# Destination scores of two graph-attention layers: spread over the partitions by two transfers through memory instead of by TensorE transposes

## The chip, the cores and the metric

The kernel runs on one core of a Trainium2 chip. A core has five engines with queues of their own: TensorE (PE, matrix products and transposes), VectorE (DVE), ScalarE (ACT), GpSimd (POOL) and SyncE (SP, which here only issues transfers). They work out of SBUF, an on-chip memory of 128 partitions; TensorE writes into the eight banks of PSUM, 2 KB a partition each; inputs and outputs lie in HBM, and 16 DMA engines move data between HBM and SBUF. An engine executes its own queue in order and waits on semaphores for the others.

The metric is the time of one execution on the device in microseconds (us).

## The reference

Four layers of graph attention are applied to 32 graphs of 512 nodes with 256 channels, all in float32, with one adjacency matrix for all. Each layer ends in a residual and a layer norm.

```python
# layer 0 ("a" in the kernel): additive attention, one head
h = x @ W
s1 = einsum('bnf,f->bn', h, a1);  s2 = einsum('bnf,f->bn', h, a2)
e = leaky_relu(s1[:, :, None] + s2[:, None, :], 0.2)
attention = softmax(where(adj > 0, e, NEG_BIG), axis=-1)
x = layernorm(x + elu(attention @ h))
# layer 1 ("b"): transformer block, 8 heads of 32 channels, masked dot-product attention
# layer 2 ("c"): additive attention again, 4 heads of 64 channels
e = e_src[:, :, None, :] + e_dst[:, None, :, :]       # each of shape (graph, node, head)
e = where(e >= 0, e, 0.2 * e);  attn = softmax(where(mask, e, NEG_INF), axis=2)
x = layernorm(x + elu(einsum('bijh,bjhd->bihd', attn, q)))
# layer 3 ("d"): bilinear attention, e = leaky_relu((x W1) (x W2)^T), then relu
```

In layers a and c the score of a pair is a sum: one number of the source node i plus one number of the destination node j. In a tile with 128 sources on the partitions and 512 destinations along the free dimension, the source's number is one value a partition. The destination's is a whole row of 512 values that every partition needs alike. How this row gets onto all partitions is what is changed.

## The kernel before

**Tiling.** A graph's 512 nodes are four blocks of 128 (`NB`), taken in two halves (`F`). The projection `prepare` (L733) yields `v`, with nodes on partitions: 256 channels, then a source score and a destination score per head. Destination score of head h is the column `C + H + h` of `v`.

**Layers a and c** (`Gat.attend`, L741). For each head the column of each node block is given to TensorE as a broadcast operand (128 equal columns) and transposed against the identity (L752 to L757): four transposes fill a PSUM bank `dst` [128, 512], whose rows are all the same. `masked` (L637) on VectorE then makes, for each of the four source blocks, `t = dst + neg`, with `neg` the bfloat16 mask in SBUF, and the row maximum. `leaky_softmax` adds the source score and applies the slope (L666) and the exponential (L672) on ScalarE. The tiles `t` are transposed on TensorE (`turn`, L549), copied from PSUM (`copied`, L492 on ScalarE or L494 on VectorE, as the planner decides), and multiplied with `v`: L807 in layer a and d, L561 in layers b and c.

**Forms of the TensorE array.** L561 uses column tiles 32 or 64 wide ("columns"), L853 (scores of layer b) row tiles of 32 ("rows"), everything else the full array ("full").

**Order.** No engine's order is written by hand. Each piece of work is given to `Plan.op` with its cost per engine, what it writes and reads, and a `lag`. `Plan.order` runs a list scheduler over all of them with up to four graphs in flight (`WINDOW`), starts on each engine the fitting piece with the best key, and emits the instructions in that order. The key is made of the graph's age (`AGE`), the length of the work behind it, an urgency by engine and stage (`URGENT`; "c3" is stage 3 of layer c) and, on TensorE, a weight for a change of form (`SWITCH`, `SWITCH_WEIGHT`). Buffers have a tag and a number of slots (`BUFS`); a piece starts only when its slots are free. `port=True` keeps a VectorE piece from starting while the planner thinks GpSimd is busy; of the VectorE pieces only the layer norms' last step (L621) has it.

**GpSimd** does residual additions (L629), the power for the norms (L609) and three additions or products of layer b (L914, L915, L918). **SyncE** issues all transfers: weights at the start, then for each graph two halves of `xT`, one `x` (L340) and two output stores (L1041).

Of the kernel before, what the change touches and what calls it, by code (L numbers as in the profile page):

```python
# [14 lines left out]
ALU = mybir.AluOpType  # L15
AX = mybir.AxisListType
PSUM = bass.MemoryType.PSUM

# [4 lines left out]
SLOPE = 0.2  # L25


BUFS = dict(t=18, pT=8, x=6, xT=3, v=5, qk=4, y=5, e=2, n=2, nT=2, hT=2, oT=4, small=8)


WINDOW = 4
# [5 lines left out]

AGE = {"PE": 51, "ACT": 138, "DVE": -107, "POOL": 461, "SP": 20}  # L40
URGENT = {
    "PE": {"a0": -417, "a1": 491, "a2": -867, "b0": -448, "b1": 197, "b2": 839, "c0": -557, "c1": -258, "c2": 203, "d0": -909, "d1": -511, "d2": -1186, "a3": 1287, "a4": 1218, "b3": -47, "b4": 169, "c3": 2234, "c4": 712},
    "ACT": {"a0": -671, "a1": 422, "a2": 770, "b0": 459, "b1": 253, "b2": 93, "c0": 729, "c1": 136, "c2": -360, "d0": 573, "d1": -523, "d2": -1234, "a3": 806, "a4": -162, "b3": 370, "b4": 340, "c3": 698, "c4": -390},
    "DVE": {"a0": -247, "a1": 1195, "a2": 496, "b0": 1368, "b1": 273, "b2": -132, "c0": -1160, "c1": 19, "c2": 666, "d0": -845, "d1": -1056, "d2": -1458, "a3": 1297, "a4": 438, "b3": -527, "b4": 175, "c3": 138, "c4": 1482},
    "POOL": {"a0": -896, "a1": -817, "a2": 582, "b0": 3, "b1": -713, "b2": 227, "c0": -148, "c1": -607, "c2": 1624, "d0": 582, "d1": 1022, "d2": -1512, "a3": -446, "a4": 431, "b3": 270, "b4": 1342, "c3": 708, "c4": 734},
    "SP": {},
}

SWITCH = {"full": {"rows": 0.1, "columns": 0.1}, "rows": {"full": 0.12, "columns": 0.12}, "columns": {}}
SWITCH_WEIGHT = 661


S_HEADS = 4
# [42 lines left out]
class Plan:  # L99
# [7 lines left out]
    def op(self, where, issue, writes=(), reads=(), takes=(), lag=0.0, port=False, form="full"):  # L107

        o = Op(len(self.ops), self.graph, where, issue)
        o.lag = LATENCY + lag
        o.port, o.form = port, form
        o.stage = self.stage
        self.ops.append(o)
        for buf in takes:
            if not buf.users and buf.tag is not None:
                o.takes.append(buf)  # L120
                self.bufs.append(buf)
                buf.users.append(o)
        for what, write in [(w, True) for w in writes] + [(r, False) for r in reads]:
            buf, cells = what if isinstance(what, tuple) else (what, None)
            if not buf.users and buf.tag is not None:
                o.takes.append(buf)
                self.bufs.append(buf)
            if not buf.users or buf.users[-1] is not o:
                buf.users.append(o)
            for c in range(len(buf.writer)) if cells is None else [cells]:  # L130
                if buf.writer[c] is not None:
                    o.after.add(buf.writer[c])
                if write:
                    o.after.update(buf.readers[c])
                    buf.writer[c], buf.readers[c] = o, []
                else:
                    buf.readers[c].append(o)
        o.after.discard(o)

    def order(self):  # L140
# [85 lines left out]
        while events:  # L226
# [28 lines left out]
            for e in URGENT:  # L255
# [3 lines left out]
                for o in ready.get(e, {}).values():  # L259
                    key = o.graph * AGE[e] - o.rank - URGENT[e].get(o.stage, 0)  # L260
                    if e == "PE":
                        key += SWITCH_WEIGHT * SWITCH[form].get(o.form, 0.0)
                    key = key, o.n
# [29 lines left out]
def gnn_stack(  # L293
# [4 lines left out]
    nc = tc.nc  # L298
    B, N, C = x.shape
    P = 128  # L300
    NB = N // P
    NC = C // P
    H1, D1 = 8, C // 8
    H2, D2 = 4, C // 4
# [6 lines left out]
    work = ctx.enter_context(tc.tile_pool(name="work", bufs=2))  # L311
    small = ctx.enter_context(tc.tile_pool(name="small", bufs=8))
    psum = ctx.enter_context(tc.tile_pool(name="psum", bufs=8, space=PSUM))


    plan = Plan()
    op = plan.op
    PE, ACT, DVE, POOL, SP = "PE", "ACT", "DVE", "POOL", "SP"
# [4 lines left out]
        return b  # L323

    def buf(tag, shape, name, cells=1, dtype=F32):
        return Buf(work, shape, tag, BUFS[tag], name, cells, dtype)

    def tiny(tag, shape, name, cells=1):
        return Buf(small, shape, tag, BUFS["small"], name, cells)

    def bank(shape, name, cells=1):
        return Buf(psum, shape, "ps", 8, name, cells)

    def block(i):
        return slice(i * P, (i + 1) * P)
# [9 lines left out]
    ident = const.tile([P, P], F32, name="ident")  # L345
# [141 lines left out]
    def copied(n, dst, ps, writes, reads):  # L487


        def issue(e):  # L490
            if e == ACT:
                nc.scalar.copy(dst(), ps())  # L492
            else:
                nc.vector.tensor_copy(dst(), ps())  # L494

        op({ACT: 0.03 + n * 0.00087, DVE: 0.06 + n * 0.00106}, issue, writes, reads)
# [57 lines left out]
    def weighted(pv, oT, pTs, v, lo, D, us):  # L554

        def issue(e):
            for j in range(NB):
                for h, pT in enumerate(pTs):  # L560
                    nc.tensor.matmul(  # L561
                        pv[h * D : (h + 1) * D], lhsT=v[:, j, lo + h * D : lo + (h + 1) * D],
                        rhs=pT[:, j], start=(j == 0), stop=(j == NB - 1), skip_group_check=True,
                    )

        op({PE: us}, issue, [pv], [v] + pTs, [oT], form="columns")
# [66 lines left out]
    def masked(s, t, top, at, i):  # L633


        def issue(e):
            nc.vector.tensor_tensor_reduce(  # L637
                out=t[:], in0=s[:], in1=neg[:, i], scale=1.0, scalar=LOWEST, op0=ALU.add,
                op1=ALU.max, accum_out=top[(slice(None),) + at],
            )  # L640

        op({DVE: 0.61}, issue, [t, top], [s, (neg, i)])
# [73 lines left out]
    class Gat(Layer):  # L716
# [24 lines left out]
        def attend(self):  # L741
            H, D, name, v = self.H, C // self.H, self.name, self.v
            G = min(H, P // D) if H > 1 else 1
            for g in range(0, H, G):
                ts = {}
                for h in range(G):
                    dst = bank([P, N], f"{name}_dst{g}{h}")
                    for i in range(NB):
                        ts[h, i] = buf("t", [P, N], f"{name}_t{g}{h}{i}")


                    def issue(e, at=C + H + g + h, dst=dst):  # L752
                        for j in range(NB):
                            column = v[:, j, at : at + 1].to_broadcast([P, P])
                            nc.tensor.transpose(dst[:, block(j)], column, ident)  # L755

                    op({PE: 0.44}, issue, [dst], [v], [ts[h, i] for i in range(NB)])  # L757
                    if h == 0:
                        tops = [
                            tiny("top", [P, FB, G], f"{name}_top{g}{f}") for f in range(F)  # L760
                        ]
                    for i in range(NB):
                        masked(dst, ts[h, i], tops[i // FB], (i % FB, slice(h, h + 1)), i)
                for f in range(F):
                    plan.stage = name[0] + "3"
                    pTs, inv = leaky_softmax(
                        {(h, i): ts[h, f * FB + i] for h in range(G) for i in range(FB)},
                        tops[f], v, C + g, G, f, f"{name}_{g}_{f}",
                    )
                    y = self.part_y(f)  # L770
                    plan.stage = name[0] + "4"
                    if H > 1:
                        pv = bank([P, FN], f"{name}_pv{g}{f}")
                        oT = buf("oT", [P, 1, FN], f"{name}_oT{g}{f}")
                        weighted(pv, oT, pTs, v, g * D, D, 1.86)
                        copied(FN, lambda oT=oT: oT[:, 0], lambda pv=pv: pv[:], [oT], [pv])
                        ps = turned_back(oT, 1, y, f"{name}_{g}{f}")
                        op({DVE: 0.4}, scaled(y, 0, g * D, ps, inv, D), [y], [ps, inv])
                    else:
                        pv = bank([P, FB, C], f"{name}_pv{f}")  # L780
                        rows_weighted(pv, pTs[0], v, y)
                        op({DVE: 0.62}, scaled(y, 0, 0, pv, inv, C), [y], [pv, inv])
                    plan.stage = name[0] + "1"
                    if g + G == H:
                        yield f
# [308 lines left out]
```

## Time and profile before

| | |
|---|---|
| Median of 3 runs | 3526.07 us (3525.98 to 3526.36) |
| Profiled execution | 3525.66 us, its span 3523.9 us |
| Granted TensorE clock in it | 0.999 |
| L755, the transposes of destination scores | 640 |
| L549, the transposes of the softmax tiles | 7168 matmuls, 898.4 us busy |
| L637, masking in layers a, c and d | 768, 685 ns median |
| L867, masking in layer b | 1024, 649.0 us busy |
| L492 and L494, copies of softmax tiles | 1099 on ACT, 693 on DVE |
| GpSimd busy | 869.1 us, 25% |

The span reaches from the first to the last record of the profiled execution. A share in percent is of the span. Busy shares overlap, since the engines work side by side; the chain of waits is followed back from the last instruction and tells what the end waited for. In lists of groups, `ps<-ident,v` means: written `ps`, read `ident` and `v`; `x640` is the number of instructions.

### The profile page before, as it was taken

The numbers are of one execution on the slowest core, as the hardware profiler recorded it, in microseconds if no ns is written. First come the engines' busy times: TensorE is split into PE (matmuls) and PEld (weight loads), VectorE is DVE, ScalarE is ACT, GpSimd is POOL, SyncE is SP. The second block draws the span as 40 slices with busy tenths as digits, with TensorE's granted clock in tenths as the row PEclk, the third lists the DMA queues.
The fourth block names the chain that finished last, engine by engine and source line by source line (L and its number), as shares of the span: only waits on it lengthen the run. The fifth ranks groups of instructions, "written<-read, shape, count | busy, mean of one in ns | idle before, by whom it ended". The sixth has DMA issues, their size and how long they took to land.

```text
span 3523.9 us, 68878 instructions
## 1 busy us (share of the span) xinstructions
PE 3501.5 (99%) x24728; PEld 2685.4 (76%) x24728; DVE 2973.8 (84%) x8792; ACT 2807.6 (80%) x6856; POOL 869.1 (25%) x840
## 2 busy tenths in 40 slices
PE   8999999999999999999999999999999999999999
PEld 7777777778777787877878778687787877878777
DVE  7789888888888888888888888888888888888886
ACT  6798877878788787887888878887788877888786
POOL 1222222222222222222222222222222222222322
PEclk9999999999999999999999999999999999999999
DMA  3000100001000010000100001000010000100000
GB/s 95 7 2 1 37 1 19 19 1 37 1 19 19 1 37 1 19 19 1 37 1 19 19 1 37 1 19 19 1 37 1 19 19 1 37 1 19 19 7 19
DMA packets 56918, 59.41 MB, mean 17 GB/s; under 512 B 3968, under 2 KB 55808, under 8 KB 56576
## 3 DMA queue, kind: packets, MB, share of 16 engines
q1 hardware_dynamic: 56576, 55.00, 4.9%
q8 instruction: 196, 3.21, 0.4%
q14 instruction: 146, 1.20, 0.1%
HBM read 38.21 MB, written 16.78 MB: 16 GB/s over the span
## 4 chain that ended last, share of the span: by engine, by line
PE 99%; DVE 1%; ACT 0%; DMA 0%; issue 0%; SPq 0%; POOLq 0%; POOL 0%; DVEq 0%
PE ps L549 23%; PE ps L561 13%; PE ps L520 13%; PE ps L807 12%; PE ps L535 10%; PE ps L853 8%; PE ps L733 7%; PE ps L975 6%; PE ps L505 3%; PE ps L755 2%; PE ps L575 2%; DMA xT<-in_x_T 0%; SPq L340 0%; DVE st L603 0%; DVE rstd L606 0%
## 5 line engine op out<-in xcount | busy, mean ns | idle before, releaser
L549 PEld LDWEIGHTS ps<-ident,t 128*128 128x128 f32 x7168 | 805.5, 141 | 178.4 <-issue 38.7
L549 PE MATMUL ps<-ident,t 128*128 128x128 f32 x7168 | 898.4, 274 | 1.0 <-ACT t L874 0.8
L874 ACT ACTIVATE t<-t,low 128x512 f32<-128x512 f32 x1024 | 734.8, 735 | 41.5 <-DVE low L867 41.5
L492 ACT COPY pT<-ps 128x512 f32<-128x512 f32 x1099 | 594.1, 593 | 119.9 <-PE ps L549 116.4
L867 DVE CUSTOM_DVE_ANT_0 t<-ps,neg 128x512 f32<-128x512 f32 x1024 | 649.0, 686 | 46.2 <-PE ps L853 43.6
L629 POOL TENSOR_TENSOR y<-y,x 128x512 f32<-128x512 f32 x256 | 330.0, 1290 | 1371.7 <-DVE y L586 493.3
L609 POOL TENSOR_TENSOR rstd<-rstd,mhalf 128x2 f32<-128x2 f32 x384 | 297.2, 774 | 1049.1 <-DVE rstd L606 934.3
L637 DVE CUSTOM_DVE_ANT_0 t<-ps,neg 128x512 f32<-128x512 f32 x768 | 492.3, 683 | 69.9 <-PE ps L975 59.4
L672 ACT ACTIVATE t<-t,bias 128x512 f32<-128x512 f32 x768 | 544.0, 709 | 0.4
L561 PE MATMUL ps<-pT,v 128*32 128x256 f32 (+1 forms) x6144 | 486.1, 382 | 0.0
L494 DVE COPY pT<-ps 128x512 f32<-128x512 f32 x693 | 451.3, 682 | 40.1 <-PE ps L549 37.8
L807 PE MATMUL ps<-v,pT 128*128 128x256 f32 x2048 | 465.5, 379 | 0.0
L666 ACT ACTIVATE t<-t,v 128x512 f32<-128x512 f32 x640 | 418.4, 715 | 32.5 <-DVE top L637 32.4
L561 PEld LDWEIGHTS ps<-pT,v 128*32 128x32 f32 (+1 forms) x6144 | 260.4, 118 | 208.1 <-issue 22.6
L807 PEld LDWEIGHTS ps<-v,pT 128*128 128x128 f32 x2048 | 378.5, 190 | 48.2 <-issue 2.3
L853 PE MATMUL ps<-qk,qk 32*128 32x512 f32 x2048 | 291.7, 639 | 0.0
L603 DVE BATCH_NORM_STATS2 st<-y 128x6 f32<-128x256 f32 x768 | 285.2, 413 | 4.5 <-POOL y L629 3.1
L975 PE MATMUL ps<-xT,qk 128*128 128x512 f32 x512 | 241.7, 596 | 0.0
L520 PE MATMUL ps<-xT,w_qkv_sb 128*128 128x256 f32 x1024 | 230.8, 379 | 0.0
L617 DVE TENSOR_SCALAR x<-y,mv,rstd 128x256 f32<-128x256 f32 x512 | 219.3, 474 | 3.7 <-POOL rstd L609 1.9
L874 ACT ACTIVATION_READ_ACCUMULATOR t<-t,low 128x1 f32 x1024 | 214.3, 209 | 0.0
L586 DVE TENSOR_TENSOR y<-ps,inv 128x512 f32<-128x512 f32 (+1 forms) x256 | 140.9, 551 | 83.9 <-PE ps L807 72.0
(84 smaller groups left out, 4630.4 us busy)
## 6 DMA issues: line engine op xcount, KB each, us to landing
xT<-in_x_T SPq DMA_DIRECT2D x64, 256.0 KB, 3.2
x<-in_x SPq DMA_DIRECT2D x32, 512.0 KB, 4.5
out<-x SPq DMA_DIRECT2D x64, 256.0 KB, 2.2
t<-in_adj SPq DMA_DIRECT2D x4, 256.0 KB, 6.8
w_qkv_sb<-in_L_gnn_w_qkv SPq DMA_DIRECT2D x1, 768.0 KB, 7.2
w_sb<-in_L_gnn_w SPq DMA_DIRECT2D x2, 256.0 KB, 5.8
t<-in_L_gnn_W SPq DMA_DIRECT2D x2, 256.0 KB, 2.8
w_sb<-in_L_gnn_W SPq DMA_DIRECT2D x1, 256.0 KB, 2.8
```

The lines of the kernel that those rows point to most:

```text
L492: nc.scalar.copy(dst(), ps())
L494: nc.vector.tensor_copy(dst(), ps())
L520: nc.tensor.matmul(ps[:, c], lhsT=w[:, k, lo + c * P : lo + (c + 1) * P], rhs=xT[:, k, nlo : nlo + FN], start=(k == 0), stop=(k == NC - 1),)
L549: nc.tensor.transpose(ps[:, j], t[:, block(j)], ident)
L561: nc.tensor.matmul(pv[h * D : (h + 1) * D], lhsT=v[:, j, lo + h * D : lo + (h + 1) * D], rhs=pT[:, j], start=(j == 0), stop=(j == NB - 1), ...
L637: nc.vector.tensor_tensor_reduce(out=t[:], in0=s[:], in1=neg[:, i], scale=1.0, scalar=LOWEST, op0=ALU.add, op1=ALU.max, accum_out=top[(sli ...
L672: nc.scalar.activation(t[:], t[:], AF.Exp, bias=bias[:, i, h : h + 1], accum_out=total[:, i, h : h + 1])
L807: nc.tensor.matmul(pv[:, i], lhsT=pT[:, j, block(i)], rhs=v[:, j, 0:C], start=(j == 0), stop=(j == NB - 1),)
L853: nc.tensor.matmul(s[:], lhsT=q_sb[at, c, block(f * FB + i)], rhs=k_sb[at, c], start=True, stop=True,)
L867: nc.vector.tensor_tensor_reduce(out=t[:], in0=s[:], in1=neg[:, f * FB + i], scale=-1.0 / math.sqrt(D1), scalar=HIGHEST, op0=ALU.add, op1= ...
L874: nc.scalar.activation(t[:], t[:], AF.Exp, bias=low[:, i, h : h + 1], scale=-1.0, accum_out=total[:, i, h : h + 1],)
L975: nc.tensor.matmul(s[:], lhsT=hh[:, k, block(f * FB + i)], rhs=xT[:, k], start=(k == 0), stop=(k == NC - 1),)
```

## The change

- `attend` makes a tile `row` [4, 512] in DRAM (HBM) for each graph and layer. For each head, SyncE writes the column of destination scores out of `v` into one row of it, value by value (512 values of 4 bytes from 128 partitions).
- A second transfer reads that row onto all 128 partitions of a tile `dst` [128, 512], which now lies in SBUF, with three slots. It waits until the write has landed. `masked` reads this `dst`; the instruction is otherwise the same.
- The transposes of L755 and their PSUM bank are gone. The buffers `t` are claimed by the masking and no longer by the transposes.
- The planner books both transfers on SP with 0.45 us and a lag of 3.0 and 2.5 us. A buffer's list of users now also has pieces that name an already used buffer in `takes`.
- `t` has 15 slots instead of 18, `nT` 3 instead of 2, `row` 37. The reserve that is kept in SBUF for transfers that GpSimd issues is 1024 bytes a partition, given explicitly. GpSimd issues no transfers in either kernel.
- All weights of the planner (`AGE`, `URGENT`, `SWITCH_WEIGHT`) are other numbers, so the order of all work on all engines is another one.

```diff
+DRAM = bass.MemoryType.DRAM
...
-BUFS = dict(t=18, pT=8, x=6, xT=3, v=5, qk=4, y=5, e=2, n=2, nT=2, hT=2, oT=4, small=8)
+BUFS = dict(t=15, pT=8, x=6, xT=3, v=5, qk=4, y=5, e=2, n=2, nT=3, hT=2, oT=4, dst=3, row=37, small=8)
...
-AGE = {"PE": 51, "ACT": 138, "DVE": -107, "POOL": 461, "SP": 20}
+AGE = {"PE": 215, "ACT": 489, "DVE": -131, "POOL": 484, "SP": 84}
...
-SWITCH_WEIGHT = 661
+SWITCH_WEIGHT = 1043
+
+DMA_US = 0.45
+ROW_LAG = 3.0
...
             if not buf.users and buf.tag is not None:
                 o.takes.append(buf)
                 self.bufs.append(buf)
+            if not buf.users or buf.users[-1] is not o:
                 buf.users.append(o)
...
+    dram = ctx.enter_context(tc.tile_pool(name="dram", bufs=1, space=DRAM))
...
-        return Buf(work, shape, tag, BUFS[tag], name, cells, dtype)
+        return Buf(dram if tag == "row" else work, shape, tag, BUFS[tag], name, cells, dtype)
...
         def attend(self):
             H, D, name, v = self.H, C // self.H, self.name, self.v
             G = min(H, P // D) if H > 1 else 1
+
+            row = buf("row", [H2, N], f"{name}_row", H)
+            for h in range(H):
+
+                def write(e, h=h):
+                    with nc.allow_non_contiguous_dma(reason="one score of each node"):
+                        nc.sync.dma_start(
+                            out=row[h].rearrange("(i p) -> p i", p=P), in_=v[:, :, C + H + h]
+                        )
+
+                op({SP: DMA_US}, write, [(row, h)], [v], lag=ROW_LAG)
             for g in range(0, H, G):
                 ts = {}
                 for h in range(G):
-                    dst = bank([P, N], f"{name}_dst{g}{h}")
+                    dst = buf("dst", [P, N], f"{name}_dst{g}{h}")
                     for i in range(NB):
                         ts[h, i] = buf("t", [P, N], f"{name}_t{g}{h}{i}")

-                    def issue(e, at=C + H + g + h, dst=dst):
-                        for j in range(NB):
-                            column = v[:, j, at : at + 1].to_broadcast([P, P])
-                            nc.tensor.transpose(dst[:, block(j)], column, ident)
-
-                    op({PE: 0.44}, issue, [dst], [v], [ts[h, i] for i in range(NB)])
+                    def read(e, h=g + h, dst=dst):
+                        nc.sync.dma_start(out=dst[:], in_=row[h].partition_broadcast(P))
+
+                    op({SP: DMA_US}, read, [dst], [(row, g + h)], lag=2.5)
...
-    nc = bacc.Bacc("TRN2", target_bir_lowering=False, num_devices=1)
+    nc = bacc.Bacc("TRN2", target_bir_lowering=False, num_devices=1, dynamic_dma_scratch_size=1024)
```

## The prediction

> **What bounds the kernel now.** I read the page first: busy shares, then the chain.
>
> ```profile
> span 3523.9 us, 68878 instructions
> ...
> PE 3501.5 (99%) x24728; PEld 2685.4 (76%) x24728; DVE 2973.8 (84%) x8792; ACT 2807.6 (80%) x6856; POOL 869.1 (25%) x840
> ...
> PE 99%; DVE 1%; ACT 0%; DMA 0%; issue 0%; SPq 0%; POOLq 0%; POOL 0%; DVEq 0%
> ...
> q1 hardware_dynamic: 56576, 55.00, 4.9%
> ```
>
> PE is busy all the time and the chain of waits lies on it: what leaves PE's queue leaves the time, as long as its suppliers keep up. The DMA engines are nearly empty. Next, the chain in order of time, from 1000 us on (start, length, line, matmuls):
>
> ```profile
> 1005.41 0.44 PE ps L755 x4
> ...
> 1006.28 1.88 PE ps L561 x16
> 1008.16 1.92 PE ps L520 x8
> ...
> 1015.19 1.73 PE ps L520 x8
> ...
> 1027.36 3.60 PE ps L561 x32
> ```
>
> L755 is what the change removes: 0.44 us for four transposes. The rest shows a second price. Two L561 groups (64-column tiles) in a row take 3.60, one alone 1.88; so a group is 1.72 and going in costs 0.16. L520 takes 1.73, but 1.92 just after L561: coming out costs 0.19. Busy time by batch (stretches of 109.2 us, the period of the trace) shows the suppliers:
>
> ```profile
> 1000.00:1109.20 109.20, 109.20 (x679) 88.12 (x678) 93.65 (x282) 87.87 (x212) 27.49 (x27) 1.00 0.10 30
> ```
>
> VectorE (third) has 15.6 us spare in a batch, ScalarE (fourth) 21. Finally single lines and transfers:
>
> ```profile
> L637 DVE CUSTOM_DVE_ANT_0 t<-ps,neg x768: 632/685/693, 20.6 to 3503.7; 128x512 f32<-128x512 f32 x192
> L795 DVE SCALAR_TENSOR_TENSOR y<-y,e x128: 669/683/828, 38.0 to 3482.4; 128x512 f32<-128x512 f32 x128
> L944 DVE SCALAR_TENSOR_TENSOR y<-y,rstd,x x128: 471/477/1490, 120.1 to 3425.0; 128x256 f32<-128x256 f32 x128
> L629 POOL TENSOR_TENSOR y<-y,x x256: 1262/1275/1646, 38.8 to 3516.8; 128x512 f32<-128x512 f32 x128
> xT<-in_x_T SPq DMA_DIRECT2D x64, 256.0 KB, 3.2
> out<-x SPq DMA_DIRECT2D x64, 256.0 KB, 2.2
> b_sb<-in_L_gnn_b SPq DMA_DIRECT2D x1, 1.0 KB, 3.7
> ```
>
> The triples are min/median/max ns; the last number of a transfer is us from issue to landing.
>
> [...] L944 has 477 ns, but about 1485 in the 13 of 128 cases where a GpSimd add (L918) had begun just before, and L629 goes to 1646. [...] here L637 (one PSUM input) and L795 (all SBUF) are 685 and 683, so I take no gain from the new source. [...] So a write of one score column is 512 descriptors of 4 bytes.
>
> **The change part by part.**
>
> 1. *Transposes gone.* 640 at L755. Their starts lie 109.1 ns apart in the trace: 640 × 0.1091 = 69.8 us off PE (160 groups × 0.44 from the chain says the same). They sit throughout the chain.
>
> 2. *PE's order anew.* New weights and three fewer t buffers reorder everything. Laying the two instruction orders side by side and counting changes of tile form (full; rows, L853; columns, L561): full to rows 249 before, 226 after; full to columns 147, 251; columns to full 203, 226; rows to full 193, 251; rows to columns 60, 5; columns to rows 4, 30. In all 856 against 989. Prices from the starts of successive matmuls: into rows or columns 0.093; a further 0.051 when a 64-column group is entered from full (79 before, 124 after); columns to full or rows 0.10; rows to full 0.005; and after any return to full a second gap of 0.056 before transposes or 0.104 before other matmuls (266 and 130 before, 346 and 131 after). Before: 23.2 + 13.7 + 4.0 + 20.5 + 1.0 + 0.4 + 14.9 + 13.5 = 91. After: 21.0 + 23.3 + 6.3 + 22.8 + 1.3 + 3.0 + 19.4 + 13.6 = 111. So +19.4 us. As a test of the method, start plus all matmuls at their undisturbed spacing plus these prices give 3506 for before, and real gaps 7 more; the last matmul starts at 3515.
>
> 3. *Two transfers in the place of a transpose.* 160 writes and 160 reads on SP, which computes nothing. An issue occupies SP for about 0.43 us (the records' durations); 320 × 0.43 = 138 us of an idle queue. Traffic: 160 × 256 KB = 42 MB more, against 55 MB at 4.9%: no load. What counts is latency. Write: a store lands in 2.2 with 256 descriptors of 1 KB; the 4-byte packets of the column loads at 16 us pass at about 100 in 0.1 us over all engines, so 512 need 0.5 to 0.7; I take 2.5. [...] Read: 256 KB, like xT, 3.2. Together with 0.2 for the waits 5.9 us.
> Layer a: in the new order VectorE has 7.9 us of its own instructions between the last copy of v and the first masking that reads dst, so it doesn't wait. Layer c: four writes issue in 1.7; the first lands at 2.5, its read at about 6. From the last projection to the first masking, the instruction ahead of it (the relu, which needs the h projection) comes 6.6 + 2 × 0.48 = 7.6 later; less 0.8 for the copy of v that leaves 6.8. Hidden by 0.8 to 2 us. Later heads have 12, 24 and 30 us. Behind a late dst would wait, on VectorE, the copy of hh that the bilinear scores need. On SP behind the writes and reads come only the output stores and next x loads, some 45 us later; the reads of the third and fourth heads wait for a free dst, also long before.
> Cost in steady state 0. At the start loads land in 4 to 7 us, and in the last batches the window from v to the first transposes is 11 to 12 us and not 23: once each, 0 to 10 us; I take 4.
>
> 4. *Port lock.* The masking now reads dst and neg, both in SBUF: 640 instructions of 685 ns become liable to what L944 shows. GpSimd's long reads are 448 × 1.28 = 573 us, 16% of the span; at random 640 × 0.16 × 0.64 = 67 us of waiting. In a repeating batch of the new order three places have such a pair side by side (L636 and L933 beside the first a maskings, L929 and L930 beside the fourth, L636 between two maskings of c): about 1.05 + 0.6 + 1.2 = 2.9 us, times 32 = 93. VectorE has room: 15.6 us a batch, and the copies move: 1200 to 1011 on VectorE (-123 us at 0.65), 1686 to 1875 on ScalarE (+108 at 0.57), both then near 84%. PE sees a delay only beyond its margin. Pairing each waiting matmul of before with the instruction it waits for: median 1.5 us, a quarter under 1.0, a tenth under 0.6. A wait of 1.2 costs PE a few tenths now and then: bounds 0 and 1.4 us a batch; I take 0.25 × 32 = 8.
>
> 5. *At nothing:* the smaller GpSimd reserve (its queue moves nothing, see q1), the third nT, the user list in the planner, the eighth of PSUM no longer held by dst (cover in either direction, PE has no gap to win).
>
> Sum: 3523.9 - 69.8 + 19.4 + 4 + 8 = 3485.5 span. The profiled execution took 3525.66, 1.8 more than its span; the median shown, 3526.07, is 0.4 above that. So 3485.5 + 2.2 = 3488.
>
> **Rivals.**
> *The lock reaches PE.* If 0.8 us of the 2.9 a batch gets through (26 us in place of 8): 3506. For it: a quarter of the margins are under 1 us. Against: before already has lock waits in L944, L940 and the norms and PE shows no gap for them.
> *Slow single-element writes (slower).* If a 4-byte write lands in 7 us, the c chain is 10.5 to 11 against 6.8 plus a margin of 1: 3.2 us a batch stops VectorE, then PE: 3488 + 102 = 3590. It decides from about 1.2 us a batch, a write of some 5 us. For it: b_sb, 256 elements, took 3.7, though behind other loads. Against: its packets took 0.6.
> *The transfers are hidden, and the order's losses eat the rest:* start and end cost 20 and the lock 20: 3516, or up to no change.
>
> **How the numbers follow.** Forecast 0.64 (own range 3475 to 3498), lock 0.22, slow writes 0.09, the last 0.05. The range 3474 to 3512 takes in the first and most of the second. 0.2% is 7 us, about what a measurement can tell: faster (under 3519) 0.64 + 0.20 + 0.02 = 0.86; slower 0.09 + 0.01 = 0.10; between 0.04.
>
> **What would show it.** PE busy near 3430 us, PE still 97% or more of the chain; no waits of VectorE for a dst read in steady state; dst maskings with a median of 685 ns and some 50 to 100 of them above 1 us; write to landing 2 to 3 us. Wrong: many PE waits that end at VectorE, waits for dst of over 1 us in each batch, or a change of form that costs other than above.

## The result, and the profile after

| | before | after |
|---|---|---|
| Median of 4 runs | 3526.19 us (3525.98 to 3526.36) | 3863.64 us (3853.05 to 3864.56) |
| Ratio | | 1.095, 95% interval 1.0931 to 1.0969 |
| Span of the profiled execution | 3523.9 us | 3861.4 us |
| Granted TensorE clock in it | 0.999 | 0.962 |

The change makes the kernel 9.5% slower. The forecast was 3488 us, in a range of 3474 to 3512. The first lines of the page of after: span, busy time by engine, the chain by engine and by line, the DMA queue.

```profile
span 3861.4 us, 67738 instructions
...
PE 3592.8 (93%) x24088; PEld 2657.5 (69%) x24088; DVE 2871.3 (74%) x8618; ACT 2908.5 (75%) x7030; POOL 880.1 (23%) x840
...
q1 hardware_dynamic: 164096, 97.29, 10.2%
...
PE 62%; DMA 20%; DVE 9%; ACT 6%; issue 3%; SPq 0%; POOL 0%; POOLq 0%; DVEq 0%; ACTq 0%
PE ps L556 15%; DMA row<-v 12%; PE ps L822 9%; PE ps L568 9%; PE ps L527 8%; PE ps L542 7%; DMA dst<-row 7%; PE ps L868 6%; DVE t L644 3%; PE ps L990 3%; ACT t L673 2%; DVE t L882 2%; PE ps L740 2%; ACT t L679 2%; PE ps L512 2%
```

Two things are new. The chain that was 99% PE is now 62% PE and 20% transfers, nearly all of it in two tiles: 12% the write `row<-v`, 7% the read `dst<-row`. The queue is still nearly empty (10.2%), so this is latency and not load. And PE executes 640 instructions fewer than before, yet its busy time rose from 3501.5 to 3592.8 us.

The waits of after (engine, tile and line, what was waited for: us in total, times, longest us):

```profile
DVE t L644 <- DMA dst<-row: 331.4, 61, 14.8
...
ACT t L673 <- DVE top L644: 286.9, 145, 13.2
...
PE ps L990 <- ACT qk L499: 99.1, 27, 4.5
```

61 waits are about two in each of the 32 batches. VectorE stops in the masking (L644; L637 before), ScalarE stops behind it for the maxima of that masking (L673), and PE stops at the bilinear scores (L990; L975 before). One batch shows how they hang together. First SyncE in the timeline of after (start, length, line, transfer; the issues' times, not the landings'):

```profile
1906.08 0.37 SPq L757 DMA_DIRECT2D row<-v  x1
1914.20 0.34 SPq L770 DMA_DIRECT2D dst<-row  x1
1923.71 2.01 SPq L757 DMA_DIRECT2D row<-v  x4
1931.94 12.81 SPq L770 DMA_DIRECT2D dst<-row  x4
```

Layer a's write is issued at 1906.08 and its read, which waits for it, at 1914.20: the write lands after 8.1 us. The read takes 4.8 more. (This and all later landings are the time from an issue to the last step that the transfer makes on its semaphore; the write and the read of layer a here make 16 each. Some steps are missing from the traces, so a median can be off by some 0.2 us.) Layer c writes four rows at 1923.71; the first read goes at 1931.94, 8.2 later, and lands 5.3 after that. So the chains are 12.9 and 13.5 us, where the prediction had 5.9 in a room of 7.9 and 6.8. VectorE in the same stretch (the brackets hold the idle time before the instruction and what ended it):

```profile
1919.04 0.69 DVE L644 CUSTOM_DVE_ANT_0 t<-dst,neg 128x512 f32<-128x512 f32 x1 [5.18 <-DMA dst<-row]
...
1937.28 0.69 DVE L644 CUSTOM_DVE_ANT_0 t<-dst,neg 128x512 f32<-128x512 f32 x1 [4.31 <-DMA dst<-row]
```

The masking at 1919.04 starts as layer a's read lands; the second wait of the batch ends at 1937.28 with layer c's first. Together 9.5 us a batch, 304 us in 32 batches, of the 331. PE in the same stretch:

```profile
1916.60 1.94 PE L740 MATMUL ps<-wg_sb,xT 128*128 128x264 f32 x8
1922.25 6.33 PE L990 MATMUL ps<-xT,qk 128*128 128x512 f32 x8 [3.70 <-ACT qk L499]
...
1939.92 2.54 PE L990 MATMUL ps<-xT,qk 128*128 128x512 f32 x4 [2.12 <-DVE qk L501]
```

PE's next matmuls need `hh`, the copy of the bilinear projection (`qk` in these lines, after its buffers); that copy stands on ScalarE behind the late L673 (first gap) or on VectorE behind the late L644 (second). Then look at the lengths: the eight L990 take 6.33 us, some 0.79 each, and not 0.6. The busy time by stretch of after shows why (columns as before; PEclk is the third from the end):

```profile
1910.00:1920.00 10.00, 8.55 (x64) 6.39 (x56) 3.76 (x9) 4.58 (x12) 2.55 (x2) 1.00 0.07 27
1920.00:1930.00 10.00, 7.75 (x23) 4.13 (x24) 6.81 (x25) 7.91 (x22) 1.61 (x2) 0.66 0.10 1
```

After the gap PE is granted half its clock for a while: the mean is 0.66 in the second of these stretches. The L990 instructions of after have 595 ns at the median and 1223 at the most. In all of after's span the clock is at half for 292 us, in before's for 6.1 us. So a gap can cost twice, as idle time and then as slow matmuls.

### The profile page after: what moved, and what is told of

Read it like the earlier page. It is cut to its first block, busy times and chain, and to the rows that moved or that the text cites. A ratio compares the mean times of both kernels' runs of the same rounds, so it can differ in the third digit from the quotient of the medians.

```text
span 3861.4 us, 67738 instructions
## 1 busy us (share of the span) xinstructions
PE 3592.8 (93%) x24088; PEld 2657.5 (69%) x24088; DVE 2871.3 (74%) x8618; ACT 2908.5 (75%) x7030; POOL 880.1 (23%) x840
## 3 DMA queue, kind: packets, MB, share of 16 engines
q1 hardware_dynamic: 164096, 97.29, 10.2%
## 4 chain that ended last, share of the span: by engine, by line
PE 62%; DMA 20%; DVE 9%; ACT 6%; issue 3%; SPq 0%; POOL 0%; POOLq 0%; DVEq 0%; ACTq 0%
PE ps L556 15%; DMA row<-v 12%; PE ps L822 9%; PE ps L568 9%; PE ps L527 8%; PE ps L542 7%; DMA dst<-row 7%; PE ps L868 6%; DVE t L644 3%; PE ps L990 3%; ACT t L673 2%; DVE t L882 2%; PE ps L740 2%; ACT t L679 2%; PE ps L512 2%
## 5 line engine op out<-in xcount | busy, mean ns | idle before, releaser
L556 PEld LDWEIGHTS ps<-ident,t 128*128 128x128 f32 x7168 | 824.9, 143 | 286.3 <-ACT pT L499 74.1
L556 PE MATMUL ps<-ident,t 128*128 128x128 f32 x7168 | 960.7, 279 | 17.8 <-ACT t L889 6.1
L499 ACT COPY pT<-ps 128x512 f32<-128x512 f32 x1317 | 714.9, 586 | 329.5 <-PE ps L556 320.7
L882 DVE CUSTOM_DVE_ANT_0 t<-ps,neg 128x512 f32<-128x512 f32 x1024 | 649.9, 685 | 98.8 <-PE ps L868 93.0
L644 DVE CUSTOM_DVE_ANT_0 t<-dst,neg 128x512 f32<-128x512 f32 x640 | 463.7, 753 | 331.4 <-DMA dst<-row 331.4
L673 ACT ACTIVATE t<-t,v 128x512 f32<-128x512 f32 x640 | 441.5, 718 | 279.7 <-DVE top L644 279.6
L636 POOL TENSOR_TENSOR y<-y,x 128x512 f32<-128x512 f32 x256 | 338.3, 1321 | 1235.3 <-DVE y L810 687.4
L822 PE MATMUL ps<-v,pT 128*128 128x256 f32 x2048 | 478.2, 384 | 3.9 <-DVE pT L501 3.0
L990 PE MATMUL ps<-xT,qk 128*128 128x512 f32 x512 | 319.1, 768 | 172.0 <-ACT qk L499 99.1
L501 DVE COPY pT<-ps 128x512 f32<-128x512 f32 x475 | 317.8, 682 | 24.2 <-PE ps L556 21.6
L990 PEld LDWEIGHTS ps<-xT,qk 128*128 128x128 f32 x512 | 115.3, 243 | 311.0 <-issue 113.8
```

Source lines behind the costliest of these rows:

```text
L556: nc.tensor.transpose(ps[:, j], t[:, block(j)], ident)
L644: nc.vector.tensor_tensor_reduce(out=t[:], in0=s[:], in1=neg[:, i], scale=1.0, scalar=LOWEST, op0=ALU.add, op1=ALU.max, accum_out=top[(sli ...
L673: nc.scalar.activation(t[:], t[:], AF.Prelu, alpha=SLOPE, bias=0.0 if src is None else v[:, f * FB + i, src + h : src + h + 1],)
L822: nc.tensor.matmul(pv[:, i], lhsT=pT[:, j, block(i)], rhs=v[:, j, 0:C], start=(j == 0), stop=(j == NB - 1),)
L882: nc.vector.tensor_tensor_reduce(out=t[:], in0=s[:], in1=neg[:, f * FB + i], scale=-1.0 / math.sqrt(D1), scalar=HIGHEST, op0=ALU.add, op1= ...
L990: nc.tensor.matmul(s[:], lhsT=hh[:, k, block(f * FB + i)], rhs=xT[:, k], start=(k == 0), stop=(k == NC - 1),)
```

## The experiments

All kernels below are the changed one with the edit shown, unless said otherwise; `...` marks what is left out of an edit. Six of them ran only once and are given without an interval. Where SyncE alone is touched, the order of instructions on PE, VectorE, ScalarE and GpSimd is that of after. Two theories stood against each other first: L, the landing of the transfers; O, the new order and three fewer `t`.

**One contiguous write.** Two runs of 1 KB, taken from two partitions, replace the 512 values; so the scores are other values than the reference's.

```diff
-    out=row[h].rearrange("(i p) -> p i", p=P), in_=v[:, :, C + H + h]
+    out=row[h].rearrange("(i p) -> i p", i=2), in_=v[0:2, 3, 0:C]
```

> The changed kernel in the same order, each write replaced by one of the same 2 KB from v, but as two runs of 1 KB in place of 512 values of 4 bytes (so the scores are other values); the read waits for it as before. If the size of the pieces makes the write slow, it lands in about 2.2 us, like an output store, and the chain write plus read falls from 12.6 us to about 7: waits for dst under 100 us, time 3490 to 3580 us. If any round trip through memory costs 8 us, nothing changes: 3864 us and 8 us to landing.

Measured: 3510.86 us, ratio to before 0.9956 (0.994 to 0.9972). The waits of the masking for `dst`, 331.4 us in after, are now:

```profile
DVE t L644 <- DMA dst<-row: 8.8, 2, 6.6
```

The clock at half falls from 292 to 22 us. Reads land in 3.2. So the whole loss against this kernel, 350.4 us of span (3861.4 - 3511.0), comes from the form of the write: 226.5 of it PE idle (268.6 against 42.1) and 123.9 PE busy for longer (3592.8 against 3468.9). The two traces have the same matmuls in the same order; 112 of the 123.9 us lie on those that touch a stretch at half the clock. So theory O falls.

**The read doesn't wait for the write.** It takes input values (2 KB) instead of `row`; the scores are other values. All writes are still made.

```diff
-    nc.sync.dma_start(out=dst[:], in_=row[h].partition_broadcast(P))
+    nc.sync.dma_start(out=dst[:], in_=x[0, 0:2].rearrange("r c -> (r c)").partition_broadcast(P))
```

> The changed kernel in the same order of all engines, but the broadcast reads take 512 values of the input x in place of the row just written, so no read waits for a write (the scores are then other values; the writes are still made). Theory L (latency: dst lands too late, mostly because a write of 512 single values takes some 8 us to land): a read is on its way as soon as SP gets to it and lands in 4 to 5 us, below the 6.8 and 7.9 us that the order leaves; waits of VectorE for dst fall from 331 us to under 60 and the time to 3480 to 3530 us. Theory O (the new order and the lock between VectorE and GpSimd cost the time, the waits for dst are only where it shows): the time stays above 3750 us.

Measured: 3809.09 us, 1.0801 (1.078 to 1.0823). By its own numbers L fails here. The trace shows what was left out of it: a read issued right behind the writes lands after 8.0 us in layer a and 12.9 in layer c (medians; up to 15.0); one with no write ahead of it in 3.1. Waits of the masking for `dst` of this kernel:

```profile
DVE t L644 <- DMA dst<-in_x: 292.2, 58, 16.4
```

The slow write holds up what is queued behind it, too. A missing wait doesn't help as long as the write is ahead.

**What makes the write slow: number, size or place of its pieces?** Four kernels. The first has 512 pieces of 512 bytes (channels of `v`, of which 2 KB are read back), the second 128 pieces of 4 bytes (only the first node block; the read repeats it four times). In both the scores are other values. The expectation of the second has two cases: first a price for each piece, then a price of the write whatever their number.

```diff
-row = buf("row", [H2, N], f"{name}_row", H)
+row = buf("row", [H2, NB, P, P], f"{name}_row", H)
-    out=row[h].rearrange("(i p) -> p i", p=P), in_=v[:, :, C + H + h]
+    out=row[h].rearrange("i p c -> p i c"), in_=v[:, :, 0:P]
...
-    nc.sync.dma_start(out=dst[:], in_=row[h].partition_broadcast(P))
+    nc.sync.dma_start(out=dst[:], in_=row[h, 0, 0:NB].rearrange("p c -> (p c)").partition_broadcast(P))
```

> The write keeps its 512 pieces, but each is 512 bytes (128 channels of a node, 256 KB in all, the same for every head); the read takes the first 2 KB of it. The scores are other values than the reference's. If the number of pieces is what costs, the write lands in 8 us or more and the time stays near after's 3864. If the size of a piece below 512 bytes is what costs, it lands in about 2 to 3 us, as the output stores do, and the time is 3500 to 3540; 42 MB more of traffic could bring up to some 30 us on top through reads and stores that share the queue.

```diff
-    out=row[h].rearrange("(i p) -> p i", p=P), in_=v[:, :, C + H + h]
+    out=row[h, 0:P].rearrange("(p i) -> p i", i=1), in_=v[:, 0, C + H + h : C + H + h + 1]
...
```

> The write takes the scores of the first node block alone: 128 pieces of 4 bytes in place of 512; the read then takes 128 values, repeated four times over the row (512-byte pieces, four times as many). The scores are other values than the reference's. Time per piece (each 4-byte piece costs about 13 ns of its own somewhere behind the packets): a single write lands in about 1.6 + 6.5/4, some 3 to 3.5 us, and the kernel is near 3530 unless the reads in smaller pieces take more than 5 us. [...] a single write still lands in 7 to 8 us, the waits for dst stay above 200 us and the time above 3750.

Measured: 3521.32 us with long pieces, a single write landing in 2.24 (the median of writes with no other close by, as for all single writes from here on; after itself 8.29). 3608.86 with a quarter of the pieces, a single write still landing in 7.76. So the number of pieces isn't it. (The 3608.86 are below the expectation: with a block's column alone the write needn't wait for the other copies of `v`, and the waits for `dst` come to 115 us. Its reads, in more pieces, take 9.2 at the median. Only the landing of the write is taken from this run.)

That leaves small pieces as such, or small pieces side by side. The third kernel puts the 512 values 64 bytes apart. The gaps are filled first with input values by one transfer a layer, and 2 KB are read back (other values again). The fourth is its control, the same with a last dimension of 1 in place of 16, so that the values lie side by side again, and a fill of `x[0, 0:8]`.

```diff
-row = buf("row", [H2, N], f"{name}_row", H)
+row = buf("row", [H2, N, 16], f"{name}_row", H)
+    if h == 0:
+        nc.sync.dma_start(
+            out=row[:].rearrange("h n k -> (h n k)").rearrange("(a b) -> a b", b=C), in_=x[0, 0:128]
+        )
-    out=row[h].rearrange("(i p) -> p i", p=P), in_=v[:, :, C + H + h]
+    out=row[h, :, 0].rearrange("(i p) -> p i", p=P), in_=v[:, :, C + H + h]
...
```

> The 512 pieces of 4 bytes go 64 bytes apart (a row of 32 KB) and not side by side; since the gaps must hold something, each layer's row is first filled with input values by one transfer in pieces of 1 KB, which the first write waits for; the read takes the first 2 KB. The scores are other values than the reference's. If pieces that fall into the same 64 bytes hold each other up, a single write lands in 2.2 to 3.5 us, and with some 2.5 us for the fill the chains are 8 to 9 us: 3530 to 3650. If every 4-byte piece has a fixed long landing, a single write lands in 7 to 9 us and the time is above 4000, since the fill comes on top of after's chain.

> The control of the run before it: the same fill (8 KB) and wait, but the 4-byte pieces side by side as in the change. The scores are those of the reference. Both theories: the write after the fill lands in 8 us, the chains are some 2.2 us longer than after's, and the time is above after's 3864, near 3950 to 4100 (32 x 2 chains x 2.2 us = 141 us, and clock lost).

Measured: 3522.89 us apart, 3882.86 side by side. A single write lands in 1.81 and in 8.11. SyncE of the kernel with the values apart, then its waits, then the waits of the control:

```profile
1953.78 0.37 SPq L761 DMA_DIRECT2D row<-v  x1
1956.76 0.34 SPq L774 DMA_DIRECT2D dst<-row  x1
...
1966.85 2.01 SPq L761 DMA_DIRECT2D row<-v  x4
1968.90 13.60 SPq L774 DMA_DIRECT2D dst<-row  x4
```

```profile
DVE t L644 <- DMA dst<-row: 14.6, 5, 9.0
```

```profile
DVE t L644 <- DMA dst<-row: 343.0, 61, 17.0
```

The same 512 packets of 4 bytes, from the same partitions, by the same queue: 1.81 against 8.11 us, by where their targets lie alone. (The control lies below its 3950, since the fill lands 4.3 us or more ahead of the write, but for five early ones, and lengthens no chain.) It fits that a quarter of the pieces takes as long: they lie just as close. Why neighbours are slow is open: the trace doesn't show the memory's inside. How near they must be isn't shown either: distances between 4 and 64 bytes weren't tried, and with the distance the whole row grew from 2 to 32 KB.

**Two other ways to write.** In the first, row and masking are in the order (partition, block), so that the four values of one partition are neighbours:

```diff
-    out=row[h].rearrange("(i p) -> p i", p=P), in_=v[:, :, C + H + h]
+    out=row[h].rearrange("(p i) -> p i", p=P), in_=v[:, :, C + H + h]
...
```

> The changed kernel with the row in DRAM in node order p then i, so that the four values of a partition lie side by side and neighbouring partitions share a stretch of memory; same order, same 512 pieces of 4 bytes; the masking reads a permuted view. If the writes are slow because different DMA engines write into the same short stretch of memory, the landing falls to 2 to 5 us and the time to 3510 to 3650 us. If each small write to DRAM has its price, landing stays near 8 us and the time near 3864 us.

Measured: 3932.22 us; a single write 6.76. The strided view that the masking needs makes it slower in its turn, so only the write is compared: it gains 1.5 us of the 6.5 that lie between 8.29 and 1.81, and still has sixteen values in 64 bytes. The group of that masking in this kernel (min/median/max ns):

```profile
L648 DVE CUSTOM_DVE_ANT_0 t<-dst,neg x640: 984/1091/2097, 36.6 to 3875.5; 128x512 f32<-128x512 f32 x160
```

In the second, `row` lies in SBUF, on the partition of the head, with four slots, in the same order and with the same masking.

```diff
-    return Buf(dram if tag == "row" else work, shape, tag, BUFS[tag], name, cells, dtype)
+    return Buf(work, shape, tag, BUFS[tag], name, cells, dtype)
...
```

> The changed kernel with the row in SBUF (one partition, node order p then i, four slots) in place of DRAM; same order of all engines, still 512 values of 4 bytes a write; the masking reads dst through a permuted view. Theory H (memory outside the chip is slow to confirm small writes): the write lands in 2 to 3 us and nothing queues behind it; the read has a single source partition and may take 4 to 10 us; time 3500 to 3700 us depending on that. Theory D (512 descriptors are slow by themselves, whatever they are written to): the write still lands in about 8 us, time 3800 us or more.

Measured: 4299.33 us. A single write lands in 3.33, against 6.76 in memory in the same order, so most of the slowness of 512 values side by side goes with the memory. But the read now comes from one partition: 11.1 us alone, 19.6 at the median and up to 31 when others are under way.

**The planner's share.** It books the write with a lag of 3.0 and the read with 2.5. With what they take:

```diff
-ROW_LAG = 3.0
+ROW_LAG = 7.5
...
-op({SP: DMA_US}, read, [dst], [(row, g + h)], lag=2.5)
+op({SP: DMA_US}, read, [dst], [(row, g + h)], lag=4.3)
```

> The changed kernel with the planner told what the trace shows: lag 7.5 us for the write (3.0 before) and 4.3 for the read (2.5). Theory L: the planner puts other graphs' work ahead of the maskings; waits for dst fall below 100 us and the time to 3470 to 3580 us, unless 15 t buffers do not hold enough work, then 3600 to 3750. Theory O: no gain beyond 100 us, 3760 us or more.

And the kernel before, transposes and all, with after's `AGE`, `URGENT`, `SWITCH_WEIGHT`, `t=15` and `nT=3`:

> The kernel before, with its transposes of the scores on TensorE, but with the new weights of the planner and t=15, nT=3. Theory L: the weights and buffers are harmless, 3520 to 3580 us. Theory O: 3700 us or more, with PE waiting for VectorE and ScalarE.

Measured: 4287.36 us, 1.216 (1.214 to 1.218), and 4146.38 us, 1.1758 (1.1734 to 1.1781). Both are outside their expectations, and neither has after's order, so they say nothing on its cause. With other lags the waits for `dst` do fall, to 127.6 us, but PE then waits 202.8 us in its transposes for ScalarE's exponentials. They fit the view that the weights suit one set of costs only. Whether weights fitted to a write of 8 us would do better wasn't tried.

**A mended version.** VectorE transposes the last 32 columns of each node block once a graph and layer (32 x 32 squares), so that a head's scores lie in 16 runs of 32 values; the write moves 16 pieces of 128 bytes.

```diff
-row = buf("row", [H2, N], f"{name}_row", H)
+row, tiles = buf("row", [H2, N], f"{name}_row", H), {}
...
+    lo = C + 2 * H - 32
+    if h == 0:
+        tiles[name] = work.tile([P, NB, 32], F32, tag="turned", name=f"{name}_turned", bufs=2)
+        nc.vector.transpose(tiles[name][:], v[:, :, lo : lo + 32])
+    turned = tiles[name]
+    at = C + H + h - lo
...
-    out=row[h].rearrange("(i p) -> p i", p=P), in_=v[:, :, C + H + h]
+    out=row[h].rearrange("(i b q) -> b i q", b=4, q=32),
+    in_=turned[at : at + 97 : 32],
```

> The changed kernel with one VectorE transpose of 32 x 32 blocks for each graph and layer ahead of the writes, so that a write is 16 runs of 32 values (128 bytes) in place of 512 single values; correct scores, same order otherwise. If the number of pieces sets the landing, it falls to 2 to 3.5 us and the time is that of the contiguous write plus next to nothing: 3505 to 3540 us, waits for dst under 40 us. [...]

Measured: 3513.46 us (3511.68 to 3515.42), ratio to before 0.9964 (0.9951 to 0.9976). It is 9% faster than after and, by 0.4%, than before, with the reference's scores. Its page, then SyncE in one batch:

```profile
span 3513.1 us, 67814 instructions
...
PE 3469.2 (99%) x24088; PEld 2608.8 (74%) x24088; DVE 2905.6 (83%) x8682; ACT 2899.1 (83%) x7030; POOL 890.1 (25%) x840
...
PE 96%; DVE 1%; ACT 1%; DMA 1%; issue 0%; SPq 0%; POOL 0%; POOLq 0%; DVEq 0%; ACTq 0%
```

```profile
1947.15 0.53 SPq L763 DMA_DIRECT2D row<-a_turned  x1
1948.80 0.33 SPq L777 DMA_DIRECT2D dst<-row  x1
1959.54 2.19 SPq L763 DMA_DIRECT2D row<-c_turned  x4
1961.85 12.73 SPq L777 DMA_DIRECT2D dst<-row  x4
```

Layer a's read follows its write by 1.65 us in place of 8.1, and lands in 3.0. The 64 transposes cost VectorE 0.31 us each, 20 us in all beside 600 us of idle time, and the waits for `dst` are 8.6 us.

## Why the prediction failed

- **Transposes and changes of form (parts 1 and 2): right in their sum.** Neither was measured alone. -69.8 and +19.4 are -50.4, or 1.58 us a batch: the period should fall from 109.2 to 107.6. The chain of the kernel with the contiguous write, which has after's order, repeats every 107.77:

```profile
786.89 6.91 PE ps L822 x32
...
894.66 6.91 PE ps L822 x32
```

  One sign was wrong whatever the write did: "PE busy near 3430" is before's 3501.5 less 69.8, but the records count a change of form as busy (before's stretch of 109.20 us is busy for 109.20). Less 50.4 it is 3451, and 3468.9 were measured.

- **Landing of the write (part 3): the step that failed.** 2.5 us were taken, and 7 in the rival with slow writes; 8.1 to 8.3 were measured, and 8.2 to 9.6 for the four of layer c. The step added the time of the packets (0.5 to 0.7, and they do pass within 0.4) to the landing of a store in pieces of 1 KB. But in the batch shown the 512 packets of 4 bytes, one a value, have all passed at 1907.4, and the last step of the semaphore comes at 1914.18. So 6.8 us lie between the last packet and the report of the landing, where the sum had only what a store in pieces of 1 KB needs for all of its landing, 2.2; in the batch shown of the kernel with the values 64 bytes apart it is 0.9 (last packet at 1955.8, last step at 1956.70). With it fell the cost of 0 in steady state: both chains overrun their room. Nothing in the trace of before writes neighbouring 4-byte pieces to memory: the prediction had slow writes as a rival, but weighed it by numbers that came from other kinds of transfer.
- **Landing of the read:** 3.2 taken, 4.8 and 5.3 measured in the chains of the batch shown. With a write of few pieces it is 3.0 to 3.4 in the same places (contiguous, or runs of 32), so this excess, too, goes with the write in single values; by what way isn't shown, since layer a's read is issued only after its write has landed.
- **The slow-write rival: right in kind, too small in size.** It had the place (layer c's masking, behind it the copy of `hh`), and was given 0.09. It priced layer c's delay alone, 3.2 us a batch or 102 us. Measured: layer a's chain overruns as well, 9.5 us a batch of VectorE's time, and on PE 226.5 us idle. Of the other 123.9 us, 112 are the clock, a term that no case had. The 51 half-clock stretches of after all start on one grid of 3.41 us, and all but the last are whole multiples of it. In the step of the grid just before, PE was idle for 2.0 us or more in 50 of the 51 cases (1.6 in one); of the 991 other steps at full clock after PE's first matmul, only two had 2.0 us, and none more. A gap of 2.12 us, much less than a step, was followed by half the clock (the second L990 above; the mean clock is 1.00 in the ten us before 1940 and 0.83 in the ten after).
- **Start and end:** 4 us taken, some 28 measured in the kernel with the contiguous write. Two stretches tell most of it; the one of that kernel is first, before's second:

```profile
3400.00:3500.00 100.00, 85.77 (x470) 61.27 (x468) 69.66 (x202) 66.06 (x156) 18.12 (x18) 0.93 0.07 22
```

```profile
3400.00:3500.00 100.00, 99.76 (x591) 77.10 (x590) 81.90 (x252) 74.18 (x180) 25.98 (x26) 1.00 0.05 17
```

  Second column, PE busy: 14 us more are lost there, 4 in the first 200 us and about 2 in the stretches beside this one; the clock, at half for 15.7 us longer, takes up to 8 more. Which of the order's choices does it was not tested. In the mended kernel the largest such wait is 8.0 us, of transposes of x (L512) for the last step of a layer norm (L624), and not for a `dst`.
- **Maskings held up by GpSimd (part 4): right.** 67 to 93 us of waiting on VectorE were worked out; 66.7 us of excess over the median of 685 ns stand in the dst maskings of the kernel with the contiguous write (89 of 640 above 1 us), and 46 in those of after. There 58 are above 1 us, and each of them began while an addition or product ran on GpSimd (L636, L929, L930, L933; L629, L914, L915, L918 before). It hardly reaches PE: 107.77 against 107.63 is 4.5 us in 32 batches, for 8 taken, and that difference holds every other error of the sum as well.
- **Without the write**, then, the sum holds: 3523.9 - 69.8 + 19.4 + 28 + 4.5 = 3506, for a span of 3511.0; 5 us stay open. The forecast of 3488 missed the kernel with a fast write by 23 us, most of it start and end; it missed the real one by 376, all but those 23 of it the write.

## What to carry to other kernels

Price a transfer by where its pieces land and when the landing is reported, not by its bytes or by the time its packets pass; single elements that fall side by side into memory were the dear case (8.11 us to landing against 1.81 apart), and a turn on chip that gave runs of 128 bytes removed it for 0.31 us a graph and layer. Where the trace holds no transfer of the kind that a change adds, let the range reach well beyond the nearest row, and add what is queued behind it. And where PE bounds the kernel, count a wait that reaches PE as a gap and, if it leaves PE idle for some 2 us within 3.41, as ahead of 50 of the 51 half-clock stretches here, a second time as the clock that is lost afterwards.

## What the hardware showed that was not expected

- 512 single writes of 4 bytes: 8.11 us to landing side by side, 1.81 when 64 bytes apart, 3.33 into SBUF side by side; 128 of them side by side 7.76; 512 pieces of 512 bytes 2.24. Shortness alone cost nothing here: the pieces that are 64 bytes apart are as short.
- A read queued behind such writes, without any dependence on them, landed after 8.0 us (one write ahead) and 12.9 (four).
- A broadcast of 2 KB from one SBUF partition to 128 took 11.1 us alone, and from memory 3.0 for the same 256 KB.
- The masking with a view of 16 bytes stride took 1091 ns at the median in place of 684.
- PE's clock fell to half for whole steps of 3.41 us (50 of the 51 stretches of after). In none of the kernels did a step after PE's first matmul with more than 2.02 us of idle time keep the full clock. Less came ahead of some drops, which the traces don't explain: 18 of the 65 drops of the kernel before with after's weights followed less than 2.0 us, the least 0.7.
